# Moving the parting of a mixture's weights from the end of an attention and mixture kernel to the middle of its attention, with other edits to the first batch's expert products

## The chip, the cores and the metric

The kernel runs on one core of one Trainium2 chip. The metric is the device time of one execution in microseconds (us). A profile of one execution, taken by the hardware profiler, goes with it. PE is TensorE, ACT ScalarE, DVE VectorE, POOL GpSimd; SP is the engine whose queue issues the transfers.

## The reference

Input `x` has 4 batches of 512 tokens of 256 features. Each batch is layer-normed and modulated, goes through 16 heads of causal attention, and is added back with a gate. It is then normed and modulated again and goes through a mixture of eight experts with top-2 routing.

```
h = layernorm(x) * (1 + ca) + sa
x = x + ga * attention(h, W_K, W_Q, W_V, W_O)          # 16 heads of 128
h = layernorm(x) * (1 + cb) + sb
d = h @ down_w + down_b                                # 256 -> 128
probs = softmax(h @ router_w + router_b - 1e-7 * cost) # 8 experts, hidden 128..512
gate = softmax(top-2 of probs)
out = sum over k, e:  gate_k * (gelu(gelu(d * mask_ke) @ w1_e + b1_e) @ w2_e + b2_e)
out = out + 0.1 * (gelu(gelu(d) @ shared_w1 + shared_b1) @ shared_w2 + shared_b2)
y   = out @ up_w + up_b + gelu(h) @ core_w + core_b
x = x + gb * y
```

An expert that isn't chosen still gives the product of `gelu(b1)`, a constant that the kernel works out once per expert and takes off.

## The kernel before, in words

**Products in parts.** Most products are made of three passes (`mm3`, lines 134 to 136). Each operand is kept as a rounded part `hi` (type float32r) and a rest `lo`, and PE adds lo*hi, hi*lo and hi*hi. A product of whole float32 operands is one call, which the trace shows as two records. A weight is loaded by `load_unit` into a staging buffer (tag `stage`, two buffers that take turns), then POOL copies it into `hi` (L194) and subtracts to get `lo` (L142). The last and largest tensors of this kind are the mixture's units, named in `UNITS`: `down`, `first0` to `first4` (the experts' w1, four blocks of 128 columns each), `second0` to `second2` (twelve of the twenty blocks of w2), `core` and `shared`. Eight blocks of w2 (`whole`) and `up` are used whole. A unit lies in one of the ten buffers of tag `wu`, or in a work buffer that is free by then.

**Attention.** 64 steps, "heads 0 to 63", go through the order group of four heads, batch, head in the group. In each step PE makes one head's scores `ps` (four row blocks), the next head's projections `pq` and `pk`, values `pv`, the output projection `po` of an older head, and the weighted values `pz` of the head three steps back. DVE adds the mask and takes the minimum (L456), ACT makes the exponentials (L466), POOL divides (L471), DVE transposes blocks of 32 (L480, L486, tile `T`), and the result goes through DRAM and back: four transfers `moved<-T` (L492), then, when they have landed, `aT<-moved` (L496). Two steps later ACT rounds it into `aTh` (L503), POOL subtracts (L142), and PE uses it in `pz`.

**Mixture.** After a batch's last head, `norm_batch`, `modulate` and `route` run beside the steps that follow. `route` (L585 to L646) is a chain of small DVE operations on 32 partitions with three ACT operations in it. Batches 0 and 1 use Exp there, batches 2 and 3 make the same from Tanh. Exp is in another function table of ACT than Gelu, and Tanh goes with both. So the first gelu, that of `before_chunks(0)` (L720), is placed behind the exponentials of the last head and of both routings. `all_ffn` then runs, batch after batch, the 20 blocks of the experts and one shared block: `first` makes `ph` (w1, three passes), a gelu `hid`, and for the twelve parted blocks a rounding `ah` on ACT (L789) and a rest `al` on DVE (L142); `second`, three blocks behind, adds `acc` (w2). At an expert's end `expert` (L829) scales by a routing row `spread`, which SP has loaded from `gates_e`, and POOL adds (L833). `idle_output` (L684) makes the constants with batch 0. The remaining `po` and `pz` of heads 60 to 63 lie between batch 0's blocks.

**What sets the order.** PE's order is the program's. The order on every other engine and on SP's queue comes from the scheduler, which plans with its own timeline; on the chip each engine and the queue then work in that fixed order, one after the other. `later`, `LATE_UNITS` (which unit is loaded at which step after the last head) and `issue_after` give the places in the program.

Of the kernel before, what the change touches and what calls it, by code (L numbers as in the profile page):

```python
# [46 lines left out]
def runs(blocks):  # L47
# [40 lines left out]
PAIRS = 10  # L88
X = PAIRS * R
X_LAST = PAIR_AT[NT - 1] * R  # L90
LAG = 3
FFN_LAG = 3
FFN_OUT = 6
# [1 line left out]
BEFORE3 = 4  # L95
EARLY = 2

LATE_UNITS = (
    ("first3", "wu", 0),
    ("core", "T", 2),  # L100
    ("second2", "wu", 4),
    ("first4", "wu", 4),
    ("shared", "aTh", 5),
    ("up", "vf", 6),
)

# [1 line left out]
def adaln_attention_moe_kernel(  # L108
# [67 lines left out]
            nc.sync.dma_start(to[:, at : at + a.shape[-1]], a)  # L176
            at += a.shape[-1]

    def load_unit(src, nm: str, early: bool = False, tag: str = "wu"):

        st = work.tile([P, 512], F32, tag="stage", name=f"st_{nm}")
        src = src if isinstance(src, list) else [src]
        n = sum(a.shape[-1] for a in src)
        st = st[:, :n]
        load_runs(st, src)
        if tag == "wu":
            u = const.tile([P, 2, 512], F32R, tag=tag, name=nm, bufs=10)
        else:
            u = work.tile([P, 2, 512], F32R, tag=tag, name=nm)
        hi, lo = u[:, 0, :n], u[:, 1, :n]  # L190
        if early:
            nc.scalar.copy(hi, st)
        else:
            nc.gpsimd.tensor_scalar(hi, st, 1.0, 1.0, ALU.mult, ALU.mult)  # L194
        rest(nc.gpsimd, lo, st, hi)
        return hi, lo
# [11 lines left out]


    gb1 = const.tile([P, NCH], F32, tag="gb1", name="gb1")  # L210
    gb1p = const.tile([P, NCH, 2], F32R, tag="gb1p", name="gb1p")

    def load_wf(u: str, tag: str = "wu"):
        blocks, in_parts = UNITS[u]
        src = [wf[:, at * P : (at + n) * P] for at, n in runs(blocks)]
        if in_parts:
            wf_u[u] = load_unit(src, f"wf_{u}", tag=tag)
            return
        pool, bufs = (const, 10) if tag == "wu" else (work, 3)
        t = pool.tile([P, len(blocks) * P], F32, tag=tag, name=f"wf_{u}", bufs=bufs)  # L220
        load_runs(t, src)
        wf_u[u] = t


    sc_e = small.tile([P, DC, B], F32, bufs=1, tag="silu_e", name="sc_e")
# [8 lines left out]
    b1 = ct[:, C_B1:C_B2]  # L234
    with tc.issue_after(exp_c.ins):
        nc.scalar.activation(gb1, b1[:, :NCH], AF.Gelu)
        nc.scalar.copy(gb1p[:, :, 0], gb1)
    rest(nc.gpsimd, gb1p[:, :, 1], gb1, gb1p[:, :, 0])
    load_wm(0)
    wqk_u[0] = load_unit(wqk[0], "wqk0", True)  # L240
    wv_u[0] = load_unit(wv[0], "wv0", True)
# [325 lines left out]
    def route(b: int):  # L567

        n = S // R

        def each(a: bass.AP) -> bass.AP:

            return a.unsqueeze(2).to_broadcast([R, n, E])

        def row(a: bass.AP) -> bass.AP:

            return a.unsqueeze(1).to_broadcast([R, n, E])

        def t2(nm):
            return small.tile([P, n], F32, tag=f"r_{nm}", name=f"r_{nm}_{b}", bufs=1)[:R]  # L580

        pl = psum.tile([P, S], F32, tag="pj", name=f"pl_{b}", bufs=3)[:R]
        parts = [(c, a) for c in range(DC) for a in h2T[b]]
        for i, (c, a) in enumerate(parts):
            nc.tensor.matmul(  # L585
                pl, lhsT=rw[:, c], rhs=a[:, c, :], start=i == 0, stop=i == len(parts) - 1
            )
        lt = work.tile([P, S], F32, tag="stage", name=f"lt_{b}")[:R]
        nc.vector.transpose(lt, pl)
        lt3 = lt.rearrange("p (j e) -> p j e", e=R)  # L590
        lg = small.tile([P, n * E], F32, tag="r_lg", name=f"r_lg_{b}", bufs=1)[:R]
        lg = lg.rearrange("p (j e) -> p j e", e=E)
        nc.vector.tensor_tensor(lg, lt3[:, :, :E], lt3[:, :, E : 2 * E], ALU.add)

        ex, s, hot1, gt = (
            lt[:, i * n * E : (i + 1) * n * E].rearrange("p (j e) -> p j e", e=E) for i in range(4)
        )
        nc.vector.tensor_tensor(lg, lg, row(rbias[:R]), ALU.add)
        m, sm, f, g1, g2 = (t2(nm) for nm in ("m", "sm", "f", "g1", "g2"))
        desc = rt[:R, R_DESC - R_ROUTER : R_DESC - R_ROUTER + E]  # L600

        def top(hot):


            nc.vector.tensor_reduce(m, lg, AX.X, ALU.max)
            nc.vector.tensor_tensor(lg, lg, each(m), ALU.subtract)
            nc.vector.scalar_tensor_tensor(s, lg, 0.0, row(desc), op0=ALU.is_ge, op1=ALU.mult)
            nc.vector.tensor_reduce(f, s, AX.X, ALU.max)
            nc.vector.tensor_tensor(hot, s, each(f), ALU.is_equal)

        def exp(to, a, spare):


            if b < 2:
                nc.scalar.activation(to, a, AF.Exp)
                return
            nc.scalar.activation(to, a, AF.Tanh, scale=0.5)
            nc.vector.tensor_scalar(spare, to, -1.0, 1.0, ALU.mult, ALU.add)
            nc.vector.reciprocal(spare, spare)
            nc.vector.scalar_tensor_tensor(to, to, 1.0, spare, op0=ALU.add, op1=ALU.mult)  # L620

        top(hot1)
        exp(ex, lg, gt)
        nc.vector.tensor_reduce(sm, ex, AX.X, ALU.add)
        nc.vector.reciprocal(sm, sm)
        nc.vector.scalar_tensor_tensor(lg, hot1, -BIG, lg, op0=ALU.mult, op1=ALU.add)
        top(gt)


        exp(g1, m, g2)  # L630
        nc.vector.scalar_tensor_tensor(g1, g1, 1.0, sm, op0=ALU.subtract, op1=ALU.mult)
        last_exps["route"] = nc.scalar.activation(g1, g1, AF.Tanh, scale=-0.5).ins
        nc.vector.tensor_scalar(g2, g1, -0.5, 0.5, ALU.mult, ALU.add)
        nc.vector.tensor_scalar(g1, g1, 0.5, 0.5, ALU.mult, ALU.add)
        nc.vector.tensor_tensor(hot1, hot1, each(g1), ALU.mult)
        nc.vector.tensor_tensor(gt, gt, each(g2), ALU.mult)


        ge = s.rearrange("p j e -> p (j e)")
        nc.vector.tensor_tensor(  # L640
            ge.rearrange("p (e j) -> p j e", e=E), hot1, gt, ALU.add
        )
        turned_gt = ex.rearrange("p j e -> p (j e)")
        nc.vector.transpose(turned_gt, ge)
        gates_e = dram.tile([E, S], F32, tag=f"gates_e{b}", name=f"gates_e_{b}")
        nc.sync.dma_start(  # L646
            gates_e.rearrange("(k a) (j r) -> (a j) k r", a=R // n, r=R),
            turned_gt.rearrange("p (k r) -> p k r", r=R),
        )
        routed[b] = gates_e  # L650
# [4 lines left out]
            wf_u["shared"], 0, P  # L655
        )

    def w2(i: int):

        if i == NCH:  # L660
            return part(wf_u["shared"], P, P)
        if i in WHOLE:
            return wf_u["whole"][:, ts(WHOLE.index(i), P)]
        k = PARTED.index(i)
        return part(wf_u[f"second{k // 4}"], (k % 4) * P, P)


# [2 lines left out]

    def idle_output(e: int, mine: list[int]):

        pc = psum.tile([P, 2], F32, tag="pj", name=f"pc_{e}", bufs=3)
        products = []
        for i in mine:
            w = w2(i)
            if i in WHOLE:
                products.append((pc[:, :1], w, gb1[:, PLACE[i] : PLACE[i] + 1]))
            else:
                products += [(pc, a, gb1p[:, PLACE[i], :]) for a in reversed(w)]  # L680

        products.sort(key=lambda p: p[0].shape[-1], reverse=True)
        for n, (o, w, m) in enumerate(products):
            nc.tensor.matmul(o, lhsT=w, rhs=m, start=n == 0, stop=n == len(products) - 1)  # L684
        if products[0][0] is pc:
            nc.vector.tensor_reduce(idle[:, e : e + 1], pc, AX.X, ALU.add)
        else:
            nc.vector.tensor_copy(idle[:, e : e + 1], pc[:, :1])

    def constant():  # L690

# [39 lines left out]
    class Mixture:  # L731
# [23 lines left out]
        def first(self, k: int, at: int):  # L755
# [11 lines left out]
            )  # L767
            mm3(ph, w1(k), self.hidden_in, True, True)
            bias = b1[:, NCH:] if e == E else b1[:, PLACE[k] : PLACE[k] + 1]
            if k in WHOLE:  # L770
                tag = "aTh" if b and WHOLE.index(k) % 3 == 2 else "qh"
                hid = work.tile([P, S], F32, tag=tag, name=f"hid_{b}_{k}")
                recent["hidden"] = nc.scalar.activation(
                    hid, ph, AF.Gelu, bias=bias
# [18 lines left out]
        def second(self, k: int, act, s: slice = slice(0, S)):  # L793
# [10 lines left out]
                    bufs=1 if mine else 3,  # L804
                )
            acc = self.accs[e, s.start]
            if k in WHOLE:
                nc.tensor.matmul(acc, lhsT=w2(k), rhs=act[:, s], start=c == 0, stop=c == n - 1)  # L808
            else:
                mm3(acc, w2(k), [a[:, s] for a in act], c == 0, c == n - 1)  # L810
            if c == n - 1:
                if b == 0 and e < E:
                    idle_output(e, list(range(k - n + 1, k + 1)))
                self.expert(e, s)

        def expert(self, e: int, s: slice):
# [181 lines left out]
    for n, (b, h) in enumerate(order):  # L998
# [17 lines left out]
                wo_u[h - 1] = load_unit(wo[h - 1], f"wo{h - 1}")  # L1016
        for f, *args in later.pop(n, ()):
            f(*args)
        if nb is not None:
            q = project(nb, nh, 0)  # L1020
        next(scores)
# [142 lines left out]
```

## Time and profile before

| | |
|---|---|
| time, median of 3 runs | 826.09 us (823.81 to 827.9) |
| profiled execution, its own time | 825.64 us |
| its span | 823.8 us |
| granted TensorE clock, mean | 0.983 |
| PE busy | 774.6 us (94%) |
| POOL busy | 531.2 us (64%) |
| DMA queue of SP, share of the 16 DMA engines | 46.1% |

Times in the trace count from the span's start. The profiled execution spends 1.84 us outside its span. A row of the groups or of the waits gives line, engine and tiles by the program's names. A record of PE overlaps its neighbours, so the pace of a series of products is read from their starts: a 128x512 product in float32r starts 0.233 us after the one ahead of it.

### The profile page before, as it was taken

What the parts mean: (1) busy time and instruction counts of PE and PEld (TensorE: products, weight loads), DVE (VectorE), ACT (ScalarE), POOL (GpSimd) and SP (SyncE); (2) the same over time, 40 slices, a digit from 0 to 9 for tenths busy, and PEclk for the clock granted to TensorE, in tenths of its full rate; (3) what the DMA queues carried; (4) which work ended last, traced back from release to release, by engine and by line L of the source; (5) the groups of instructions that cost most, each with busy time, mean ns of one, the idle gap of its engine ahead of it and who ended that gap; (6) DMA issues with size and microseconds to landing.
All of it is one profiled execution on the core that took longest, in us unless ns stands there. A gap on an engine that the chain in (4) does not pass through costs nothing. (4 is left out here: it accounts for less than half of the span.)

```text
span 823.8 us, 14059 instructions
## 1 busy us (share of the span) xinstructions
PE 774.6 (94%) x4499; PEld 675.5 (82%) x4499; DVE 611.6 (74%) x1740; ACT 495.2 (60%) x1186; POOL 531.2 (64%) x535
## 2 busy tenths in 40 slices
PE   5989999999999999999999999999985978989997
PEld 4768989999999999999999999988874856767775
DVE  5868787677777767777777777698959496795555
ACT  3656666666666666566656665666644453656663
POOL 3745566796645689665658967475656477464675
PEclk9999999999999999999999999999987998999999
DMA  7365354665554466554545645545373321222121
GB/s 231 89 206 148 115 156 128 199 171 168 147 156 129 138 191 177 159 164 139 158 130 167 183 143 160 142 143 148 111 213 92 99 76 62 66 64 67 62 81 60
DMA packets 67345, 112.05 MB, mean 136 GB/s; under 512 B 8372, under 2 KB 49604, under 8 KB 67272
## 3 DMA queue, kind: packets, MB, share of 16 engines
q1 hardware_dynamic: 67240, 111.15, 46.1%
q8 instruction: 36, 0.59, 0.3%
q14 instruction: 37, 0.30, 0.1%
q0 software_dynamic: 32, 0.02, 0.0%
HBM read 67.02 MB, written 44.11 MB: 135 GB/s over the span
## 5 line engine op out<-in xcount | busy, mean ns | idle before, releaser
L142 POOL TENSOR_TENSOR aT<-aT,aTh 128x1152 fp32r<-128x1152 f32 x64 | 171.8, 2685 | 110.4 <-ACT aTh L503 110.4
L471 POOL TENSOR_SCALAR e<-e,inv 128x128 f32<-128x128 f32 (+3 forms) x256 | 135.0, 540 | 72.2 <-DVE inv L470 70.2
L466 ACT ACTIVATE e<-e,nmax 128x128 f32<-128x128 f32 (+3 forms) x256 | 143.3, 561 | 48.9 <-DVE nmax L456 48.0
L503 ACT CAST aTh<-aT 128x1152 fp32r<-128x1152 f32 x64 | 74.0, 1156 | 136.3 <-PE pz L136 74.3
L456 DVE CUSTOM_DVE_ANT_0 e<-ps,mask 128x128 f32<-128x128 f32 (+3 forms) x256 | 122.3, 483 | 40.6 <-PE ps L450 25.9
L486 DVE STREAM_TRANSPOSE T<-e 128x384 f32<-128x384 f32 (+2 forms) x256 | 100.6, 446 | 8.4 <-POOL e L471 8.4
L134 PE MATMUL ps<-kh,ql 128*128 128x256 f32 (+2 forms) x192 | 71.0, 370 | 6.0 <-DVE nmax L456 5.4
L134 PE MATMUL pv<-wv,hTl 128*128 128x256 f32 x256 | 72.2, 282 | 0.0
L134 PE MATMUL po<-wo,zl 128*128 128x256 f32 x256 | 72.1, 282 | 0.0
L135 PE MATMUL po<-wo,zh 128*128 128x256 f32 x256 | 72.1, 281 | 0.0
L135 PE MATMUL pv<-wv,hTh 128*128 128x256 f32 x256 | 72.0, 281 | 0.0
L136 PE MATMUL pv<-wv,hTh 128*128 128x256 f32 x256 | 72.0, 281 | 0.0
L136 PE MATMUL po<-wo,zh 128*128 128x256 f32 x256 | 71.9, 281 | 0.0
L470 DVE RECIPROCAL inv<-tot 128x1 f32<-128x1 f32 x256 | 40.4, 158 | 40.1 <-ACT e L466 32.8
L833 POOL TENSOR_TENSOR oacc<-oacc,part 128x512 f32<-128x512 f32 x28 | 41.9, 1496 | 41.9 <-DVE part L829 34.8
L142 DVE TENSOR_TENSOR zl<-pz,zh 128x512 fp32r<-128x512 f32 x64 | 44.0, 687 | 32.1 <-ACT zh L521 31.2
L142 DVE TENSOR_TENSOR al<-hid,ah 128x512 fp32r<-128x512 f32 x48 | 46.8, 984 | 27.6 <-ACT ah L789 27.6
L135 PE MATMUL ps<-kl,qh 128*128 128x256 f32 (+2 forms) x192 | 65.2, 340 | 0.5 <-DVE kl L142 0.5
L134 PE MATMUL pz<-aTh,vl 128*128 128x512 f32 (+2 forms) x192 | 64.9, 338 | 0.0
L136 PE MATMUL ps<-kh,qh 128*128 128x256 f32 (+2 forms) x192 | 64.9, 338 | 0.0
L135 PE MATMUL pz<-aT,vh 128*128 128x512 f32 (+2 forms) x192 | 64.9, 338 | 0.0
L136 PE MATMUL pz<-aTh,vh 128*128 128x512 f32 (+2 forms) x192 | 64.8, 338 | 0.0
(217 smaller groups left out, 2350.5 us busy)
## 6 DMA issues: line engine op xcount, KB each, us to landing
moved<-T SPq DMA_DIRECT2D x256, 160.0 KB, 2.6
aT<-moved SPq DMA_DIRECT2D x64, 640.0 KB, 3.9
spread<-gates_e SPq DMA_DIRECT2D x32, 256.0 KB, 3.2
st_wqk<-in_wqk SPq DMA_DIRECT2D x16, 256.0 KB, 4.1
st_wv<-in_wv SPq DMA_DIRECT2D x8, 256.0 KB, 3.4
st_wo<-in_wo SPq DMA_DIRECT2D x8, 256.0 KB, 3.8
wmod<-in_wmod SPq DMA_DIRECT2D x6, 256.0 KB, 5.4
x<-in_x SPq DMA_DIRECT2D x3, 512.0 KB, 6.5
```

The lines of the kernel that those rows point to most:

```text
L134: nc.tensor.matmul(o, lhsT=wl, rhs=mh, start=start, stop=False)
L135: nc.tensor.matmul(o, lhsT=wh, rhs=ml, start=False, stop=False)
L136: nc.tensor.matmul(o, lhsT=wh, rhs=mh, start=False, stop=stop)
L142: return eng.tensor_tensor(lo, full, f32(hi), ALU.subtract)
L456: least = nc.vector.tensor_tensor_reduce(out=et, in0=ps[:, :n], in1=maskf[:, S - n :], scale=-SCALE, scalar=BIG, op0=ALU.add, op1=ALU.min, ...
L466: exp = nc.scalar.activation(et, et, AF.Exp, bias=nm[:, t : t + 1], scale=-1.0, accum_out=tot[:, t : t + 1])
L470: nc.vector.reciprocal(inv[:, one], tot[:, one])
L471: by_sum = nc.gpsimd.tensor_scalar(et, et, inv[:, one], 1.0, ALU.mult, ALU.mult)
L486: nc.vector.transpose(to[:, first : first + n], blocks[:, at : at + (n - 1) * step + 1 : step])
L503: nc.scalar.copy(hi, full)
L833: recent["added"] = nc.gpsimd.tensor_tensor(oacc, oacc, to, ALU.add).ins
```

## The change

The eleven parted units are no longer parted when they are needed. `part_wf` takes each to a staging buffer, rounds it on ACT, subtracts on POOL and writes both parts to DRAM (`wfp_...`), beside head 17 for the first, 19 for the second, 20 to 27 for the next eight and 33 for `down`. For the `second` units it also writes the whole float32. Near the end, `load_wf` loads the parts straight into the unit's tile, without staging or parting; both parts come in one transfer of 512 KB. Where and in which tile a late unit lies changes too (`LATE_UNITS`).

Batch 0's second products, and the constants of `idle_output`, use whole float32 for all twenty blocks, so `ah` and `al` fall away for twelve blocks of batch 0. After the last use of a `second` unit in batch 0, its two parts are loaded over it (`load_parts`) for batches 1 to 3.

Batch 1's routing uses Tanh as those of batches 2 and 3 do, and the first gelu stands behind batch 0's routing and the last head's exponential alone.

```diff
+LAST_USE = {f"second{u}": PARTED[4 * u + 3] for u in range(len(PARTED) // 4)}
+TO_PART = tuple(u for u, (_, in_parts) in UNITS.items() if in_parts)
+PART_AT = (17, 19, *range(20, 28), 33)
 LATE_UNITS = (
     ("first3", "wu", 0),
-    ("core", "T", 2),
-    ("second2", "wu", 4),
+    ("second2", "aTh", 2),
     ("first4", "wu", 4),
-    ("shared", "aTh", 5),
+    ("core", "wu", 4),
+    ("shared", "T", 5),
     ("up", "vf", 6),
 )
...
+    def part_wf(u: str):
+        n = len(UNITS[u][0]) * P
+        st = work.tile([P, 512], F32, tag="stage", name=f"st_wf_{u}")[:, :n]
+        load_runs(st, wf_runs(u))
+        d = parts_d[u] = dram.tile([P, 3, n], F32, tag=f"wfp_{u}", name=f"wfp_{u}")
+        if u.startswith("second"):
+            nc.sync.dma_start(d[:, 2, :], st)
+        hi = work.tile([P, 512], F32R, tag="stage", name=f"hi_wf_{u}")[:, :n]
+        nc.scalar.copy(hi, st)
+        nc.sync.dma_start(d[:, 0, :], f32(hi))
+        rest(nc.gpsimd, st.bitcast(F32R), st, hi)
+        nc.sync.dma_start(d[:, 1, :], st)
...
+        t = wf_t[u] = pool.tile([P, 2, 512], F32, tag=tag, name=f"wf_{u}", bufs=bufs)
+        wf_u[u] = t[:, 0, :n].bitcast(F32R), t[:, 1, :n].bitcast(F32R)
+        if u.startswith("second"):
+            nc.sync.dma_start(t[:, 1, :n], parts_d[u][:, 2, :])
+        else:
+            load_parts(u)
+
+    def load_parts(u: str):
+        n = len(UNITS[u][0]) * P
+        nc.sync.dma_start(wf_t[u][:, :, :n], parts_d[u][:, :2, :])
...
-            if b < 2:
-                nc.scalar.activation(to, a, AF.Exp)
+            if b == 0:
+                last_exps["route"] = nc.scalar.activation(to, a, AF.Exp).ins
                 return
...
-        last_exps["route"] = nc.scalar.activation(g1, g1, AF.Tanh, scale=-0.5).ins
+        nc.scalar.activation(g1, g1, AF.Tanh, scale=-0.5)
...
-            if k in WHOLE:
+            if k in WHOLE or (not b and k < NCH):
                 tag = "aTh" if b and WHOLE.index(k) % 3 == 2 else "qh"
+                if not b:
+                    tag = ("qh", "e")[k % 2]
...
-            if k in WHOLE:
-                nc.tensor.matmul(acc, lhsT=w2(k), rhs=act[:, s], start=c == 0, stop=c == n - 1)
+            if k in WHOLE or (not b and k < NCH):
+                nc.tensor.matmul(acc, lhsT=w2(k, b), rhs=act[:, s], start=c == 0, stop=c == n - 1)
...
+                    for u in [u for u, at in LAST_USE.items() if k - n < at <= k]:
+                        load_parts(u)
...
+        if n in PART_AT:
+            part_wf(TO_PART[PART_AT.index(n)])
```

`idle_output` loses its products in parts: it makes one whole product of one column per block, from `gb1`, and copies the sum. The tile `gb1p` with the parts of `gb1` goes, with the ACT copy and the POOL subtraction that made it.

More of the change, by code (lines that the diff above doesn't have):

```diff
@@ L177, in load_runs, with load_unit @@
             at += a.shape[-1]
-    def load_unit(src, nm: str, early: bool = False, tag: str = "wu"):
+    def load_unit(src, nm: str, early: bool = False):
         st = work.tile([P, 512], F32, tag="stage", name=f"st_{nm}")
[L182 to L190, printed above, removed]
+        nc.sync.dma_start(st, src)
+        u = const.tile([P, 2, 512], F32R, tag="wu", name=nm, bufs=10)
+        hi, lo = u[:, 0], u[:, 1]
         if early:
@@ L210, in adaln_attention_moe_kernel, with wf_runs @@
     gb1 = const.tile([P, NCH], F32, tag="gb1", name="gb1")
-    gb1p = const.tile([P, NCH, 2], F32R, tag="gb1p", name="gb1p")
+    parts_d: dict[str, bass.AP] = {}
+    wf_t: dict[str, bass.AP] = {}
+    def wf_runs(u: str):
+        return [wf[:, at * P : (at + n) * P] for at, n in runs(UNITS[u][0])]
+    def part_wf(u: str):
[10 more added lines that the diff above has]
+        nc.sync.dma_start(d[:, 1, :], st)
     def load_wf(u: str, tag: str = "wu"):
         blocks, in_parts = UNITS[u]
-        src = [wf[:, at * P : (at + n) * P] for at, n in runs(blocks)]
-        if in_parts:
-            wf_u[u] = load_unit(src, f"wf_{u}", tag=tag)
-            return
[L219 to L222, printed above, removed]
+        n = len(blocks) * P
+        pool, bufs = (const, 10) if tag == "wu" else (work, 3 if tag == "vf" else 2)
+        if not in_parts:
+            wf_u[u] = pool.tile([P, n], F32, tag=tag, name=f"wf_{u}", bufs=bufs)
+            load_runs(wf_u[u], wf_runs(u))
+            return
+        t = wf_t[u] = pool.tile([P, 2, 512], F32, tag=tag, name=f"wf_{u}", bufs=bufs)
[7 more added lines that the diff above has]
+        nc.sync.dma_start(wf_t[u][:, :, :n], parts_d[u][:, :2, :])
     sc_e = small.tile([P, DC, B], F32, bufs=1, tag="silu_e", name="sc_e")
@@ L236, in adaln_attention_moe_kernel @@
         nc.scalar.activation(gb1, b1[:, :NCH], AF.Gelu)
-        nc.scalar.copy(gb1p[:, :, 0], gb1)
-    rest(nc.gpsimd, gb1p[:, :, 1], gb1, gb1p[:, :, 0])
     load_wm(0)
@@ L656, in w1, with w2 @@
         )
-    def w2(i: int):
+    def w2(i: int, b: int):
         if i == NCH:
@@ L664, in w2 @@
         k = PARTED.index(i)
+        if b == 0:
+            return wf_t[f"second{k // 4}"][:, 1, ts(k % 4, P)]
         return part(wf_u[f"second{k // 4}"], (k % 4) * P, P)
@@ L671, in idle_output @@
     def idle_output(e: int, mine: list[int]):
[L673 to L688, printed above, removed]
+        pc = psum.tile([P, 1], F32, tag="pj", name=f"pc_{e}", bufs=3)
+        for n, i in enumerate(mine):
+            at = PLACE[i]
+            nc.tensor.matmul(
+                pc, lhsT=w2(i, 0), rhs=gb1[:, at : at + 1], start=n == 0, stop=n == len(mine) - 1
+            )
+        nc.vector.tensor_copy(idle[:, e : e + 1], pc)
     def constant():
@@ L806, in second @@
             acc = self.accs[e, s.start]
-            if k in WHOLE:
-                nc.tensor.matmul(acc, lhsT=w2(k), rhs=act[:, s], start=c == 0, stop=c == n - 1)
+            if k in WHOLE or (not b and k < NCH):
+                nc.tensor.matmul(acc, lhsT=w2(k, b), rhs=act[:, s], start=c == 0, stop=c == n - 1)
             else:
-                mm3(acc, w2(k), [a[:, s] for a in act], c == 0, c == n - 1)
+                mm3(acc, w2(k, b), [a[:, s] for a in act], c == 0, c == n - 1)
             if c == n - 1:
```

## Prediction

> **What bounds the kernel now.** I read the page, then PE's waits after 590 us, then a table of stretches, then ACT's timeline.
>
> ```profile
> span 823.8 us, 14059 instructions
> PE   5989999999999999999999999999985978989997
> PEclk9999999999999999999999999999987998999999
> ...
> PE ph L134 <- DVE ghh L723: 9.2, 1, 9.2
> PE ph L134 <- POOL wf_first L142: 7.2, 1, 7.2
> PE ptn L358 <- DVE ql L142: 3.6, 1, 3.6
> PE acc L134 <- ACT ah L789: 3.1, 1, 3.1
> PE acc L135 <- DVE al L142: 1.4, 1, 1.4
> ...
> 300.00:400.00 100.00, 100.00 (x632) 91.33 (x632) 74.84 (x237) 63.73 (x169) 69.77 (x71) 1.00 0.56 161
> 600.00:620.00 20.00, 16.39 (x89) 14.61 (x88) 10.40 (x33) 10.13 (x24) 11.34 (x12) 0.83 0.71 214
> 620.00:640.00 20.00, 10.45 (x51) 8.79 (x50) 18.83 (x55) 8.07 (x16) 12.05 (x12) 0.74 0.29 81
> 680.00:700.00 20.00, 16.79 (x73) 12.92 (x74) 13.51 (x26) 7.41 (x13) 14.74 (x13) 0.83 0.19 61
> ```
>
> PE is the bound: full from 100 to 600 us, one head per 9.18 us (first `ps` of heads 61 and 62 at 591.92 and 601.11). It waits only around the change of stage, and there its clock falls too (third column from the right, 0.74 to 0.83). ACT's timeline shows what two of the waits hang on:
>
> ```profile
> 606.38 1.15 ACT L503 CAST aTh<-aT 128x1152 fp32r<-128x1152 f32 x1 [3.96 <-DMA aT<-moved]
> ...
> 631.46 0.21 ACT L632 ACTIVATE r_g<-r_g 32x16 f32<-32x16 f32 x1 [3.66 <-DVE r_g L631]
> 631.70 1.28 ACT L720 ACT_TABLE_LOAD   x1
> 632.99 0.66 ACT L720 ACTIVATE pd<-pd,cols 128x512 f32<-128x512 f32 x1
> ```
>
> The rounding of `aTh` sits on ACT until its transfer lands, with `qh` behind it, whose rest `ql` frees the bank that PE's `ptn` wants. The first gelu stands behind batch 1's whole routing.
>
> [...] after the 3.61 us wait, 128x512 products start 0.43 us apart until 615.2 instead of 0.233. [...] here, issued by SP, 16 KB of `gates_e` takes 1.5 us, 256 KB of `out` 2.1, 256 KB of a weight 3.9. [...] here L606 takes 2.38 us beside POOL's `aT`, 0.27 without.
>
> **The change, part by part.** All against the profiled execution's 825.64 us, 0.45 below the median of 826.09.
>
> *1. First `ptn` wait.* In the changed order ACT makes head 63's `qh` and `hTh` ahead of the rounding of head 60's `aTh`, so `ql` no longer waits for the transfer: -3.6 us and the slow clock after it (609.22 to 615.2, half lost) -3.0. Late next is head 62's third exponential, but head 63's scores need its results only some 5 us later. The eight `whole` loads in 512-byte rows move three heads ahead; `first2` (512 KB) and two spreads take their place before `aT`, about as much. **-6.6.**
>
> *2. First gelu.* Wait 9.22 + 0.33 us. Now ACT has the last exponential, table (1.28), gelu (0.66), then DVE `ghh` (0.69). In the trace that exponential ends at 623.3 and the `pz` ahead of PE's wait at 625.2; with part 1 ACT's lead shrinks to some 1 us, and DVE has a routing operation (0.7) first. 1.28 + 0.66 + 0.69 + 0.7 - 1: about 2.3 us stay. Before `ghl` DVE has two routing operations and two statistics (1.3 us), another 1.4 with the step between engines. The slow clock stays[...]. 9.55 - 3.7: **-5.9** (bounds -2 and -8).
>
> *3. Parted weights.* `first4` is no longer parted late: its subtraction stood on POOL behind an addition, and its staging load on SP behind spreads that waited until 671.95. Now 512 KB come when head 61's `po` has freed the tile. -7.16, and half of the 4.2 us slow clock after 682.5, -2.1; `shared` -0.7. POOL loses 20 us here. **-10.0.**
>
> *4. Batch 0 whole.* A whole product is two records of 0.43 us, 0.86; three passes are 3 x 0.233 = 0.70. Twelve blocks: +1.9. `idle_output` keeps 40 records at about the same pace: 0. Twelve `ah` (0.62) and twelve `al` (0.67) go; only 1.4 us of it held PE. **+0.5.** `gb1p` at the start: 0, PE waits then for `sc`.
>
> *5. Routing by Tanh in batch 1.* Six small DVE operations more, and the chain now runs after the first gelu with ACT's hidden gelus and `zh` between its Tanhs. Summing DVE's row after `ghh` (about 35 operations) `zl` of head 61 comes some 12 to 14 us later, while PE reaches that `po` after 10 to 11: a new wait of 2.5 us. Batch 2's routing is unchanged, but lay under the 7.16 us wait: two gelus (blocks 14, 15) stand behind its Tanhs, PE's blocks 16 and 17 behind them: 2 us. **+4.5.** These are estimates; bounds 0 and 10.
>
> Parts 1 to 5: -6.6 - 5.9 - 10.0 + 0.5 + 4.5 = **-17.5**. The later wait of 3.1 us (batch 2's routing chain of batch 3) stays. The three reloads of `second` wait for PE's last read; behind them on SP are spreads for experts well ahead: 0.
>
> *6. Beside heads 17 to 33.* Eleven times: a load, an ACT copy (0.57), a POOL subtraction (1.3), two or three writes. In time alone it fits: per head POOL has 6.6 + 1.3 of 9.18 us, ACT 5.9 + 0.6, the DMA share goes from 0.55 to about 0.85. The order is the danger. The copies of `first2` to `core` have fixed places on ACT from the end of head 19 to head 25's last exponential: seven steps in 5.9 heads, 54 us. A step needs: load 3.9, copy 0.6, subtraction 1.3, issue 0.4, write landed 2.1 (the `out` row), for the next load's staging buffer is only then free: 8.3 us. For `second1`, `second2` and `shared`, the queue of SP lengthens it: three pieces issued and landed 4.0, raw write 0.35, four `moved` 1.76, `aT` when they have landed 2.3 + 0.34, then the write of the rest 0.35 + 2.1: 11.2 us. 4 x 8.3 + 3 x 11.2 = 66.8, so the last copy is 13 us late. The first, `first2`, holds ACT 2.7 us longer than it stood anyway. Together 15.5. Behind a waiting copy on ACT are `aTh`, `zh`, the exponentials; behind them POOL's scaling and DVE's transposes, which end 0.7 us before PE's next scores free DVE; before PE feels it there are 1.7 (transposes) to 3.6 us (`zh`) of slack. Taken: **+12**. Bounds: +0, if each write lands by the planned time; +24, if all seven steps take 11.2 and slack is 1.7 (78.4 - 54 + 2.7 - 1.7 = 25.4).
>
> Sum: -17.5 + 12 = -5.5, 825.64 - 5.5 = **820 us**.
>
> **The rivals.**
> *Parting is hidden.* For it: each engine has a quarter to a third of its time free beside the heads (300 to 400 us), and 27.8 us of ACT's waits for `aT` cost PE nothing. Against: one wait each is at most 3.4 us, these add up. +2 instead of +12: 810 us.
> *Slower: the staging chain sets the heads' pace.* One mechanism: two `stage` buffers and SP's fixed order, so each unit takes longer than a head and ACT stops for it. For it: POOL stood up to 5.94 us for a staged weight at 642 us. It decides from a loss of 17.5 us, that is when a step takes 11 us on average. At 24: 832 us.
> *Routing takes over.* Part 5 costs 10 more than is gained there, with slow clock: gain 11, loss 12: about 827 us, no change.
> *The edit doesn't do what it says*: the wait of part 1 stays, as `aT` lands behind 512 KB: 6.6 less, inside the second and third ranges.
>
> **How the numbers follow.** Likeliest, as summed, 0.45 (814 to 826); hidden 0.20 (806 to 814); staging chain 0.24 (828 to 838); routing 0.11 (822 to 831). 0.5% is 4.1 us, about what a measurement can tell from no change: faster is below 822, slower above 830. Faster: 0.31 of the first and all of the second, 0.51. Same: 0.14 of the first, 0.10 of the last, 0.03 of the third, 0.27. Slower: 0.21 + 0.01 = 0.22. The range 807 to 833 takes in most of each case and leaves out about 0.1 on each side.
>
> **What would show it.** PE's waits: `ph <- ghh` near 2 to 4 us, no wait for `wf_first` or `wf_shared`, no `ptn <- ql`; `acc` of batch 0 on one line. In 200 to 290 us: waits of `ps` or `po`, some 12 us in all; ACT copies of `hi_wf` that wait for DMA; heads 20 to 26 longer than 9.18. The forecast is wrong if the heads keep 9.18 there (810), or head 26 starts more than 17 us later than at 9.18 each (slower).

## The result, and the profile after

The changed kernel takes 824.01 us (median of 20 runs, 820.95 to 826.59) against 826.28 us for the kernel before on the same chips (20 runs, 823.81 to 828.92). The ratio is 0.9974, with a 95% interval of 0.9962 to 0.9986: 2.1 us faster, where 5.5 had been forecast. The profiled span is 822.3 us against 823.8.

The page of the changed kernel: the span, then PE's busy tenths and its granted clock in 40 slices.

```profile
span 822.3 us, 14105 instructions
...
PE   6889999999998799999999999999998898989997
...
PEclk9999999999999999999999999999999899999999
```

The hole at 600 to 700 us has become shallower. The clock's three low slices of before (8 and 7 from 597 to 638 us, 8 from 680 to 700) are now one, an 8 from 637 to 658 us. But there is a new hole, 87, in slices 13 and 14 from the left (247 to 288 us); single waits begin at 224 us. PE's waits over the whole execution (engine and line, what it waited for, us in total, times, longest):

```profile
PE ps L139 <- DVE nmax L481: 17.1, 13, 3.2
PE pt_mod L298 <- DVE sc L257: 6.4, 1, 6.4
PE po L139 <- DVE zl L147: 4.2, 2, 2.2
PE acc L139 <- ACT ah L809: 3.1, 1, 3.1
PE ph L139 <- ACT hid L793: 2.7, 2, 2.1
PE ph L140 <- DVE ghl L147: 1.9, 1, 1.9
PE ps L475 <- DVE nmax L481: 1.5, 1, 1.5
PE ph L139 <- DVE ghh L741: 0.9, 1, 0.9
```

Gone are `wf_first` (7.2), `ptn <- ql` (3.6), `al` (1.4) and `wf_shared` (0.7); `ghh` went from 9.2 to 0.9. In their place stands `ps <- nmax`, some 10 us of it in heads 21 to 29. A table by stretch (PE busy is the second number, then after the other engines the clock, DMA share and GB/s):

```profile
200.00:290.00 90.00, 78.19 (x482) 68.96 (x481) 53.87 (x176) 50.67 (x134) 55.66 (x56) 1.00 0.69 210
...
620.00:640.00 20.00, 15.29 (x93) 12.67 (x91) 16.55 (x43) 14.02 (x28) 13.95 (x11) 0.98 0.55 175
680.00:700.00 20.00, 17.26 (x80) 12.02 (x80) 14.17 (x31) 8.57 (x15) 11.46 (x10) 1.00 0.29 87
```

From 200 to 290 us PE was busy 90.00 of 90 us before, at a DMA share of 0.51; now it is busy 78.19.

ACT's timeline (start, duration, instruction, idle time before it) at the two places shown of before:

```profile
618.38 0.48 ACT L460 CAST qh<-pq 128x384 fp32r<-128x384 f32 x1
618.75 0.60 ACT L394 CAST hTh<-ptn 128x512 fp32r<-128x512 f32 x1
620.99 1.16 ACT L528 CAST aTh<-aT 128x1152 fp32r<-128x1152 f32 x1 [1.63 <-DMA aT<-moved]
...
632.22 1.28 ACT L738 ACT_TABLE_LOAD   x1
633.52 0.66 ACT L738 ACTIVATE pd<-pd,cols 128x512 f32<-128x512 f32 x1
634.11 0.29 ACT L642 ACTIVATE lt<-r_lg 32x128 f32<-32x128 f32 x1
```

`qh` and `hTh` now stand ahead of the rounding that waits for `aT`, and batch 1's routing (`lt`) behind the first gelu. The table load took 1.28 us. Each of the two traces holds four of these, two at an Exp and two at a Gelu, where ACT comes to one or goes over to the other, and none at a Tanh.

To place the time, I compare the start of each head's first `ps` in both traces (after less before): -0.86 at head 19, +6.07 at 24, +9.90 at 26, +13.31 at 27, +14.45 at 29, unchanged up to head 62 (+14.44), +7.89 at 63, and -1.5 at the end. So the heads lost **15.3 us**, head 63's start won 6.55, and the rest of the mixture 9.4. "Loss of the heads" below means this shift from head 19 to head 62, in one profiled execution.

### The profile page after: what moved, and what is told of

Read it like the earlier page. It is cut to its first block, busy times and chain, and to the rows that moved or that the text cites. A ratio compares the mean times of both kernels' runs of the same rounds, so it can differ in the third digit from the quotient of the medians.

```text
span 822.3 us, 14105 instructions
## 1 busy us (share of the span) xinstructions
PE 777.1 (95%) x4487; PEld 671.3 (82%) x4487; DVE 597.4 (73%) x1734; ACT 490.4 (60%) x1184; POOL 521.4 (63%) x523
## 5 line engine op out<-in xcount | busy, mean ns | idle before, releaser
L496 POOL TENSOR_SCALAR e<-e,inv 128x128 f32<-128x128 f32 (+3 forms) x256 | 135.7, 543 | 66.8 <-DVE inv L495 64.8
L140 PE MATMUL pz<-aT,vh 128*128 128x512 f32 (+2 forms) x192 | 65.3, 340 | 0.0
L141 PE MATMUL pz<-aTh,vh 128*128 128x512 f32 (+2 forms) x192 | 65.3, 340 | 0.0
L139 PEld LDWEIGHTS ps<-kh,ql 128*128 128x128 f32 x192 | 36.6, 191 | 28.0 <-DVE nmax L481 19.9
```

Of the source, the lines that this page charges most:

```text
L139: nc.tensor.matmul(o, lhsT=wl, rhs=mh, start=start, stop=False)
L140: nc.tensor.matmul(o, lhsT=wh, rhs=ml, start=False, stop=False)
L141: nc.tensor.matmul(o, lhsT=wh, rhs=mh, start=False, stop=stop)
L496: by_sum = nc.gpsimd.tensor_scalar(et, et, inv[:, one], 1.0, ALU.mult, ALU.mult)
```

## The experiments

Each ratio is to the kernel before on the same chip; rows are best compared by their ratios.

| kernel | median us | ratio to before, 95% interval | loss of the heads, us |
|---|---|---|---|
| changed kernel | 824.01 | 0.9974 (0.9962 to 0.9986) | 15.3 |
| spread | 822.88 | 0.9958 (0.9937 to 0.9979) | 12.9 |
| raw writes elsewhere | 822.39 | 0.9943 (0.9926 to 0.9960) | 12.0 |
| before + partings | 837.16 | 1.0127 (1.0107 to 1.0148) | 14.3 |
| other buffers for `hi` | 823.07 | 0.9948 (0.9927 to 0.9969) | 14.8 |
| copies pinned, two heads apart | 813.73 | 0.9859 (0.9822 to 0.9897) | 4.2 |
| copies pinned, dense | 820.85 | 0.9940 (0.9920 to 0.9960) | 13.9 |
| before + transfers alone | 839.99 | 1.0158 (1.0119 to 1.0198) | 13.6 |
| before + engine work alone | 825.25 | 1.0001 (0.9979 to 1.0022) | 0.0 |
| before + bytes, no waits | 825.20 | 0.9993 (0.9978 to 1.0007) | 1.4 |
| before + transfers, placed | 828.43 | 1.0029 (1.0015 to 1.0043) | 2.9 |
| all placed, dense | 819.42 | 0.9918 (0.9890 to 0.9946) | 7.1 |
| best version | 809.76 | 0.9806 (0.9768 to 0.9843) | 0.2 (1.8 from head 7) |
| changed, routing undone | 828.56 | 1.0024 (1.0005 to 1.0043) | 15.4 |
| before + routing edit | 821.48 | 0.9949 (0.9929 to 0.9970) | 0.2 |

### First: density, chain or bytes?

**Spread**: `PART_AT = (17, 20, 22, 24, 26, 35, 37, 39, 41, 43, 51)`.

> The changed kernel with the eleven partings further apart: beside heads 17, 20, 22, 24, 26, 35, 37, 39, 41, 43 and 51 instead of 17, 19, 20 to 27 and 33. Same transfers, copies, subtractions and bytes. Theory (the two staging buffers and SP's fixed order make a step longer than a head, so it is the density that costs): heads 19 to 29 lose at most 3 us against the kernel before instead of 15.3, the tail keeps its gain of 16, about 810 us. Rival (the bytes, or the added work of ACT and POOL, cost some 1.4 us per unit wherever it stands): the loss stays near 15 us, spread over heads 17 to 52, about 824 us.

Measured 822.88: the theory missed. The trace shows why the run says less than it was meant to: nothing ties a parting to its head but the buffers, and the scheduler moved the copies forward, to heads 17.2, 19.2, 20.0, 21.0, 21.7 and 35.2, 36.3, 37.5, 38.1, 38.6. Two runs of five took the place of one of ten: 4.9 us lost in the first, 7.6 in the second, and 0.4 at heads 54 to 56.

**Raw writes elsewhere**: the raw write leaves `part_wf`; beside heads 8 to 10 instead:

```
+        if n in (8, 9, 10):
+            u = f"second{n - 8}"
+            parts_d[u] = dram.tile([P, 3, 512], F32, ...)
+            load_runs(parts_d[u][:, 2, :], wf_runs(u))
```

> The changed kernel with the raw write of the three second units taken out of the parting: the whole float32 copies are made from DRAM to DRAM beside heads 8, 9 and 10. Partings stay beside heads 17, 19 to 27 and 33. Theory (length of a step by SP's order): SP no longer waits in a second unit's step for the pieces to land before it may issue the four moved and the aT; the steps after second0, second1 and second2, 11.7, 11.5 and 10.9 us in the changed kernel, come down towards the 8.3 of a first unit, so the heads lose 6 to 9 us less than 15.3, about 816 to 818 us. Rival (bytes or engine work): the same bytes and one more read, no gain, about 824 us.

Measured a loss of 12.0 instead of 15.3. So the raw writes carry 3.3 us of the loss, half of what was expected, and the greater part has another cause.

**Before + partings**: `part_wf` and its call added to the kernel before.

> The kernel before with only the partings beside heads 17, 19 to 27 and 33 added; the parts are written to DRAM and not read, the mixture still stages and parts its weights as before. It measures the heads' loss by itself. Theory: heads lose 14 to 16 us, with waits of ps at the same places as in the changed kernel, the tail keeps all its waits (ghh 9.2, wf_first 7.2, ptn 3.6): 826 + 15, about 841 us. Rival (part of the 15.3 us comes from the changed order around it, and the tail edits are worth less than 16): the loss is well below 15, about 832 us.

Measured 837.16 and 14.3: the loss belongs to the partings, not to the order around them.

**Other buffers for `hi`**: its `tag="stage"` becomes `tag="spread"`.

> The changed kernel with the rounded part of each unit put in another buffer pair (the tag of the spreads, two buffers unused during the heads) instead of in the second staging buffer. Same transfers, bytes, work and places. Theory (the rotation of two buffers): the next unit's load needs no longer the landing of the hi write and of the lo write of the unit just ahead, only that of the unit before it; a step falls from about 9.5 us on average below the 9.18 of a head, and the loss at heads 19 to 29 from 15.3 to under 6 us, 809 to 815 us. Rival (SP's order alone holds the loads back, or bytes or work do): the loss stays at 12 to 15 us, 821 to 824 us.

Measured 14.8, as the rival had it: freeing one buffer of the rotation changes nothing that the trace shows. The copies moved forward to heads 16.7 to 23.4, and the same loss fell into fewer heads.

After these four, five kernels lost 12 to 15 us each, as a fixed cost per unit would have it. The next four were made to take that apart.

### Second: ACT's copies, transfers or work?

**Copies pinned, two heads apart**: `PART_AT = (18, 20, 22, 24, 26, 35, 37, 39, 41, 43, 51)`, the call moves behind the head's exponentials, and

```
-        nc.scalar.copy(hi, st)
+        with tc.issue_after(exp):
+            nc.scalar.copy(hi, st)
```

> The changed kernel with each ACT copy of a parting queued behind the last exponential of its head, and the heads two apart (18, 20, 22, 24, 26, 35, 37, 39, 41, 43, 51), so that in the order no copy can be hoisted towards its load, as happened in the spread version, where ten copies stayed in two runs of five. Same transfers, bytes and work. New theory (a copy stands in ACT's fixed order where the plan has its load landed, on the chip the load lands later, and every such copy stops ACT; neither density nor bytes as such): the copies find their data, ACT's waits for the loads fall from some 24 us to under 4, the heads lose at most 3 us, about 809 to 812 us. Rival (each unit costs some 1.2 us by its transfers or its work, as five runs with 11.9 to 15.3 us would have it): 820 to 824 us.

Measured 813.73, and 4.2 us lost where the theory allowed 3: 10 us better than the changed kernel with the same bytes and work. A fixed cost per unit is refuted. Spacing and place changed together here; spacing in the program alone, as in the spread version, had not held, since the copies moved together again. The first five units cost 0.0, the three `second` units with their raw writes 2.0, and 2.0 fell at heads 53 to 55, where the loads of `down` and `first0` (512 KB) were moved in ahead of a head's `moved` and `aT`.

**Copies pinned, dense**: the same, with the heads of the changed kernel.

> The changed kernel with the copies queued behind the last exponential of their heads, at the heads of the changed kernel (17, 19, 20 to 27, 33). Tells the place in ACT's order from the spacing. If the place alone counts, nearly as good as the version with two heads between, about 811 to 814 us. If the two staging buffers can't turn within 9.18 us, each copy still waits for a load that waits for the last write: a loss of 8 to 14 us at heads 21 to 28, 817 to 823 us. Rival (bytes or work): 820 to 824 us.

Here only one copy finds its load missing for longer than 0.7 us. ACT's waits from 100 to 590 us:

```profile
ACT aTh L529 <- DMA aT<-moved: 60.6, 22, 5.3
...
ACT hi_wf_second L228 <- DMA st_wf_second<-in_wf: 3.8, 1, 3.8
```

and still the heads lost 13.9 us (its profiled execution was 2.7 us above its median). The size is that of the expectation's second case, but not its reason, a load missing at each copy. So ACT's waiting for the staged weights, which I had made the carrier of the loss, isn't needed for it: `aTh` waits instead.

**Transfers alone**, on the kernel before: no copy, no subtraction; the staged tile is written two or three times.

> The kernel before with the transfers of the partings alone, beside heads 17, 19 to 27 and 33: each unit is loaded into a staging buffer and written to DRAM two or three times; there is no ACT copy and no POOL subtraction, and nothing reads what is written. Theory (ACT's waiting copies): no engine but SP waits, so the heads lose 0 to 3 us, by SP's queue alone; 826 to 829 us. Rival (bytes, or SP held up so that aT comes late): 9 to 14 us, 835 to 840 us.

Measured 13.6 us, nearly the whole loss without any engine work: the theory in the expectation fell. **Engine work alone**, on the kernel before: `hi` and `st` are made from the mask, with no transfer.

> The kernel before with the engine work of the partings alone at the same heads: an ACT copy and a POOL subtraction per unit, from a tile that is always there (the mask) into the staging buffers, no load and no write. Theory: ACT and POOL have the room, 0 to 2 us, 826 to 828 us. Rival (work: 11 x (0.57 + 1.3) us of which most comes on the path): 5 to 12 us, 831 to 838 us.

Measured 825.25 us and a loss of 0.0. The trace of the transfers alone shows how they cost time. SP's timeline (start, duration, what it issues):

```profile
218.52 0.46 SPq L230 DMA_DIRECT2D wfp_second<-st_wf_second  x1
221.71 1.28 SPq L179 DMA_DIRECT2D st_wf_second<-in_wf  x3
223.03 2.05 SPq L511 DMA_DIRECT2D moved<-T  x4
225.25 1.14 SPq L228 DMA_DIRECT2D wfp_second<-st_wf_second  x1
226.43 0.44 SPq L229 DMA_DIRECT2D wfp_second<-st_wf_second  x1
226.92 0.48 SPq L230 DMA_DIRECT2D wfp_second<-st_wf_second  x1
228.12 0.32 SPq L515 DMA_DIRECT2D aT<-moved  x1
```

and ACT's, of the same kernel:

```profile
232.42 1.15 ACT L522 CAST aTh<-aT 128x1152 fp32r<-128x1152 f32 x1 [5.31 <-DMA aT<-moved]
```

What SP waited for from 218 to 223 us:

```profile
SPq L179 <- DMA wfp_first<-st_wf_first: 2.7, 1, 2.7
```

A load stands from 219.0 to 221.7 until an older unit's writes have landed and its staging buffer is free; the four `moved` behind it go out at 223.0, though DVE had written the last of their `T` at 216.9; three writes come between them and `aT`, and `aT` lands 4.3 us after its issue, when ACT has stood for 5.3.

### Third: bytes, or waiting in SP's queue?

**Bytes, no waits**: the same number and bytes of transfers, DRAM to DRAM, each unit's behind an `aT`:

```
+        with tc.issue_after(recent["aT"]):
+            load_runs(d[:, 2, :], wf_runs(u))
+            for k in range(3 if u.startswith("second") else 2):
+                ...
+                nc.sync.dma_start(d2, wqk[k][:, :n])
```

> The kernel before with transfers of the same number and bytes as the partings', at the same heads (17, 19 to 27, 33), but from DRAM to DRAM and with nothing to wait for: each unit's two to five (load pieces, hi, rest, raw) are queued on SP right behind the aT of the head ahead. No copies, no subtractions, nothing reads what is written; the wf pieces come from the weights, the other writes from wqk as a stand-in. Theory now (SP's queue works in order, and loads that wait for a staging buffer and writes that wait for a landing hold up the moved and aT behind them; bytes don't matter): 0 to 3 us, 826 to 829 us. Rival (the bytes themselves make moved and aT land later): 8 to 14 us, 834 to 840 us.

**Transfers, placed**: a unit's load behind the `aT` of the head ahead, its writes behind the next.

> The transfers-alone version with its places on SP's queue fixed by hand: a unit's load stands right behind the aT of the head ahead, its two or three writes a head later, again right behind an aT, so that on SP none of them waits for a landing or a buffer. Same tiles, bytes, number of transfers and density as the version that lost 13.6 us. Theory (waiting on SP): the loss falls from 13.6 to under 3 us, 826 to 829 us. Rival (bytes or number of transfers at this density): it stays above 9 us, 835 us or more.

Both came out as the theory had it: 1.4 and 2.9 us, the second just inside its bound of 3. From 200 to 290 us, first the transfers alone, then the placed ones:

```profile
200.00:290.00 90.00, 81.37 (x492) 71.93 (x491) 57.73 (x188) 50.45 (x135) 47.60 (x52) 0.98 0.68 212
```

```profile
200.00:290.00 90.00, 89.22 (x557) 80.64 (x556) 63.69 (x208) 55.29 (x148) 53.66 (x53) 1.00 0.74 225
```

The same tiles, a **higher** DMA share (0.74 against 0.68), and 7.9 us more of PE. But the two differ in more than the order. In the first the scheduler had moved the transfers forward and bunched them: ten loads from 177 to 238 us, where the placed version has them from 187 to 284. From 210 to 250 us its DMA share was 0.87 and then 0.80 (in steps of 20 us), the placed version's at most 0.78 from 190 to 290. So bunched bytes may have a part in its 13.6 us. In the changed kernel they can't have much: its share is at most 0.73 in the same steps, and its heads lost 15.3 us. So the bytes are hidden at the placed version's share, and the changed kernel's loss comes from waiting in order, not from them.

**All placed, dense**: the changed kernel with loads and writes tied to `aT`, copies to the last exponential, `hi` in the spreads' buffers, raw copies as above, at its own heads.

> The changed kernel with its partings as dense as they are (heads 17, 19 to 27, 33) but every waiting instruction placed by hand: a unit's load behind the aT of the head ahead, its ACT copy behind the last exponential of its head, both writes behind that head's aT, the rounded part in the spreads' buffers, the raw copies from DRAM to DRAM before. Theory (waits on SP's queue, not density or bytes): heads lose 0 to 3 us, 809 to 812 us. Rival (with the copies and subtractions, one unit per head is too dense even so): 817 to 824 us.

It lost 7.1 us in its profiled execution, which at 815.26 us lay 4.2 under the median; 819.42 us is where the rival, that one unit per head is too dense even so, had put it. The medians serve better here: by their ratios the two dense versions stand 11 us (copies pinned) and 9 us (all placed) above the best version below, whose heads lose next to nothing (0.9940 and 0.9918 against 0.9806). This is an estimate of what their heads lose, and their intervals overlap. Here ACT does wait at copies, 19 us in all from 100 to 590 us, since a load issued beside the writes of the unit ahead lands after the exponential that its copy is tied to:

```profile
241.41 0.62 ACT L234 CAST hi_wf_first<-st_wf_first 128x512 fp32r<-128x512 f32 x1 [2.48 <-DMA st_wf_first<-in_wf]
...
251.84 0.62 ACT L234 CAST hi_wf_second<-st_wf_second 128x512 fp32r<-128x512 f32 x1 [3.18 <-DMA st_wf_second<-in_wf]
```

So at one unit a head each of the two engines that work in order can carry a part: pinning the copies nearly ended ACT's waits for staged weights, placing everything ended most of SP's, and neither came near to the versions two heads apart. Spacing matters beside the place. That what is left in the last version is ACT's is argued from these lines; no run took both kinds of wait away at this density.

**Best version**: copies pinned, `PART_AT = (8, 10, 18, 20, 22, 24, 26, 36, 38, 40, 42)`, raw copies DRAM to DRAM.

> A version meant to beat both: the changed kernel with each copy queued behind the last exponential of its head, partings at heads 8, 10, 18, 20, 22, 24, 26, 36, 38, 40, 42, and the raw copies of the second units made from DRAM to DRAM before. The pinned and spaced version left 4 us at heads 38 to 41 (units with raw write) and 54 (down). Theory: those go, heads lose 0 to 2 us, 808 to 811 us. Rival (what is left there is bytes, or early heads have no room): 812 to 816 us.

Measured 809.76 us, 1.9% under the kernel before. Heads 17 to 62 lose nothing; 1.7 us fell at heads 9 to 11, beside the two early units. Its ACT and SP rows (100 to 590 us, and 200 to 290 us) show what slack looks like:

```profile
ACT aTh L529 <- DMA aT<-moved: 73.7, 25, 4.6
```

```profile
SPq L522 <- DMA moved<-T: 19.1, 18, 2.1
SPq L518 <- DVE nmax L482: 13.9, 4, 4.8
SPq L229 <- ACT vh L437: 10.4, 5, 2.9
```

ACT waits longer for `aT` (73.7 us) than in the changed kernel (49.3), SP waits too, and PE loses nothing by it: the total of such a row is no measure of damage.

### Fourth: what the routing edit is worth

**Routing undone** in the changed kernel (`if b < 2:` with Exp, `last_exps["route"]` on the later Tanh), and **the routing edit alone** on the kernel before.

> The changed kernel with the routing edit undone: batch 1 uses Exp again, and the first gelu stands behind the routing of both batches. Prices the prediction's steps 2 and 5 together, a saving of 5.9 less 4.5. By those steps the undone version is 1.4 us slower, 825.5 us: ph waits for ghh about 9 us again, while the new waits po <- zl (2.0) and ph <- hid (2.7) go. If the wait for the first gelu is worth its whole length: 5 us slower, 829 us. If the Tanh chain costs more than it saves, the undone version is faster, 820 us.

> The kernel before with the routing edit alone: Tanh in batch 1's routing, the first gelu behind batch 0's routing and the last exponential. By the prediction's steps 2 and 5, of which the two gelus behind batch 2's routing stay covered by the wait for first4: 5.9 less 2.5, 3.4 us faster, 822.7 us. By the run with the edit undone in the changed kernel: 4.5 us faster, 821.5 us. If its gain hangs on the other edits (head 63's qh ahead of the rounding of aTh): under 1.5 us, 825 us.

The edit alone is worth 4.2 us (ratio 0.9949), near what the undone version had led to expect and above the prediction's 3.4, and undoing it costs about as much: 1.0024 against 0.9974 is 0.5%, 4.1 us, near the case in which the wait for the first gelu counts in full. It doesn't hang on the other edits. In the undone version PE waits 9.1 us for `ghh` again; `po <- zl` near 640 us goes, but `ph <- hid` (2.7) stays.

## Why the prediction was right or wrong

| step | forecast | measured |
|---|---|---|
| 1, first `ptn` wait | -6.6 | -6.55 |
| 2, first gelu | -5.9 | waits 9.55 to 2.79: -6.8 |
| 3 to 5, weights, whole products, routing | -5.0 | about -2.6 |
| 6, beside heads 17 to 33 | +12 | +15.3 |
| start of the kernel | 0 | -0.9, differs by execution |

**Step 1** held to 0.1 us: the slow clock after the wait went with it (0.56 from 609 to 616 us before, 1.00 now).

**Steps 2 and 5.** First gelu 0.9 better than forecast, with `ghh` at 0.87 us for 2.3 and `ghl` at 1.92 for 1.4, so its sum came nearer than its parts; `zl` 2.0 for the 2.5 forecast. The slow clock stayed, as forecast, but later: before it read 0.66 from 625 to 640 us and 1.00 from 640 to 650, now 0.97 and 0.70. Together the edit was forecast at -3.4 and measured at -4.2. The two gelus behind batch 2's routing came as forecast, 2.7 us for 2. They are the price of step 3, not of the edit, since they stay when it is undone.

**Steps 3 and 4.** The waits of 7.16, 0.69 and 1.42 us are gone, and the clock from 680 to 700 us is 1.00 for 0.83. Steps 2 to 5 were to bring 10.9 and brought 9.4. Head 63 has a new wait of 0.7 us for `nmax`, `acc` one of 0.2 for `part`, and from 800 us to the end the clock reads 0.95 where it read 0.99; by estimate (0.7, 0.2, and 0.04 of 22 us) that makes about the difference, but no run isolates it.

**Step 6 is the step that failed**, by 3.3 us: its sum was mis-sized, in the slack that it took off and in what it left out behind the last copy. The lateness itself it had right. The seven steps from the copy of `first2` to that of `core` took 65.3 us (forecast 66.8), and the first copy waited 2.5 (forecast 2.7). SP and ACT of the changed kernel in the second step of a `second` unit:

```profile
231.56 1.38 SPq L181 DMA_DIRECT2D st_wf_second<-in_wf  x3
236.62 0.33 SPq L225 DMA_DIRECT2D wfp_second<-st_wf_second  x1
236.99 3.01 SPq L517 DMA_DIRECT2D moved<-T  x4
240.05 0.46 SPq L228 DMA_DIRECT2D wfp_second<-hi_wf_second  x1
242.57 0.34 SPq L521 DMA_DIRECT2D aT<-moved  x1
242.95 0.43 SPq L230 DMA_DIRECT2D wfp_second<-st_wf_second  x1
243.49 1.44 SPq L181 DMA_DIRECT2D st_wf_second<-in_wf  x3
```

```profile
236.87 0.62 ACT L227 CAST hi_wf_second<-st_wf_second 128x512 fp32r<-128x512 f32 x1
...
248.53 0.62 ACT L227 CAST hi_wf_second<-st_wf_second 128x512 fp32r<-128x512 f32 x1 [5.98 <-DMA st_wf_second<-in_wf]
```

Load to load is 11.9 us (forecast 11.2): the raw write waits for the pieces, `moved` behind it, `hi` behind `moved`, the rest behind `aT`. Head 25's last exponential, behind the last copy, started 15.8 us later than before (278.30 us for 263.41, counted from head 19 as the heads are); the step had 15.5. From these it took 3.5 us of slack, near the larger of its two figures, 3.6 and 1.7. What PE got of them, in ACT's and PE's timelines:

```profile
277.78 0.62 ACT L227 CAST hi_wf_core<-st_wf_core 128x512 fp32r<-128x512 f32 x1 [2.23 <-DMA st_wf_core<-in_wf]
278.30 0.72 ACT L491 ACTIVATE e<-e,nmax 128x512 f32<-128x512 f32 x1
...
282.26 0.44 PE L139 MATMUL ps<-kh,ql 128*128 128x384 f32 x1 [3.15 <-DVE nmax L481]
...
292.01 1.16 ACT L528 CAST aTh<-aT 128x1152 fp32r<-128x1152 f32 x1 [4.16 <-DMA aT<-moved]
```

DVE transposes head 25's weights when this exponential has come and been scaled, from 280.46 us, and only behind that, at 281.94, makes the `nmax` that PE waits for. Head 27 started 14.2 us late (13.31 + 0.86). So the slack was 1.6 us: the short path, by the transposes, counted, which the step had named and used for its bound alone. Another 1.1 us fell before head 29, after ACT had waited 4.16 us for the `aT` used at 292.01; the sum had stopped at the last copy. Lateness 0.3, slack 1.9 and what came behind it 1.1 make the 3.3 us. What made that `aT` late is open: the writes of `core` and two loads for the next heads went out ahead of its `moved`, but at 282.23 `moved` followed the end of the transposes by 0.2 us.

The danger that the step named, SP's fixed order, was the right one; that two buffers in rotation make it isn't shown, since `hi` in other buffers lost as much. The carrier that it named, copies that stop ACT, is there in the changed kernel (22 us of waits from 100 to 590 us, the longest 6.0), but isn't needed: with the copies out of the way the lateness came through `aT`. How the 15.3 us divide between the two no run shows.

**The rivals.** "Parting is hidden" argued from the free time of the engines and of the DMA: the engines' work does cost nothing (0.0) and the bytes little (1.4 and 2.9), yet the conclusion was wrong, because waits on a queue aren't counted in busy time (in the transfers alone SP stood 2.7 us before one load, with four `moved` behind it). The slower rival, steps longer than a head for which ACT stops, fits the changed kernel's trace and stopped short of its point of decision: 15.3 is under 17.5, and the steps averaged 9.3 us. (By the step's own terms 17.5 us needs steps of 10.3, not the 11 that the rival gives: 54 + 17.5 + 3.5 - 2.7 = 72.3, over seven.) "Routing takes over" is refuted: the edit gains 4.2 us.

The gain of 16.0 us after head 62 was thus nearly eaten by 15.3 us beside the heads: in the best version the same edits bring 15.65, and from head 19 on the heads take 0.2 back.

## What to carry to other kernels

When work is moved into a stretch with free engines, go through each in-order queue, the one that issues transfers first. In the transfers alone a load waited there 2.7 us for a landing, and the `moved` behind it went out 6.1 us after its `T` was written; PE lost time once the slack was used up: 13.6 us in all, 2.9 us with the same ones placed, 1.4 us with the same bytes and no waits. Tie such instructions behind ones that come late enough, and leave room between the units. Here a copy behind the last exponential of its head, with units two heads apart, lost 4.2 us, and 0.2 in the best version; the same at one unit a head lost 13.9. Left to the scheduler, copies stood up to 6.0 us ahead of their data. When a lateness is summed up, take off the slack of the shortest path that the trace shows, and follow the sum past the last instruction that was added.

## What the runs showed that was not expected

The heads lost 15.3 us in the changed kernel at a DMA share of 0.69 from 200 to 290 us, and 2.9 us with placed transfers of the same size at 0.74. Profiled executions stood up to 4.2 us from the median of their own kernel, and head 19 began from 1.7 us earlier to 1.1 later than before. A shift taken between two heads of one trace is free of the second, but not of the first: where two versions lie within some microseconds, the medians decide.
